# A planned attention stage: scoring steps ranked five tiles ahead, and the plan's durations replaced

## The chip, the core and the metric

The kernel runs on one core of a Trainium2 chip. Five engines work side by side, each with an instruction queue of its own that is worked off in order: TensorE (PE, with its weight loads shown apart as PEld), VectorE (DVE), ScalarE (ACT), GpSimd (POOL) and SyncE (SP, which here only issues transfers). They wait for each other through semaphores. The metric is the device time of one launch in microseconds, as the median of several runs.

## The reference

One transformer block with adaptive layer norm, on `x` of 2 batches x 2048 tokens x 256 features, all in f32:

```python
mod = (_silu(L0_c) @ L0_wmod).reshape(L0_c.shape[0], 6, 1, -1)
sa, ca, ga, sb, cb, gb = (mod[:, 0], ..., mod[:, 5])
ga = (2 * (ga >= 0) - 1) * jnp.maximum(jnp.abs(ga), 0.25)      # gb likewise
h = _layernorm(x, axis=-1) * (1 + ca) + sa
x = x + ga * attn(h, Wq, Wk, Wv, Wo)
h = _layernorm(x, axis=-1) * (1 + cb) + sb
x = x + gb * ffn(h, Wg, bg, Wt, bt, W1, b1, W2, b2)
```

`attn` is causal attention with two query heads of 128 that share one key and one value head, with rotary embedding on queries and keys. `ffn` is a mixture of eight experts (256 to 1024 to 256, GELU between): a softmax gate less a threshold of the token's own decides which experts a token goes to, and with which weight.

## The kernel before, in words

The work comes in two stages. `attention` (L203) does everything up to the experts' lists and a first piece of expert 0; `experts` (L1100) then runs loops on each engine over the experts' tokens, 256 at a time. The loops' main lines are L1219 (`h`, first product), L1245 (`g`, GELU) and L1210 (`y`, second product).

Attention is cut into 32 tiles of 128 tokens, which alternate between the batches in groups (4 tiles each three times, then 2, 1 and 1). A tile's number in that order is `r` (0.0 to 31.0). For each tile, `tile_steps` (L435) adds steps to a plan. In order, with the names that the profile shows:

- the load of `x` (L448, SP); its moments `sta`, `mva` (L423, L425, DVE) and `rstda` (L429, L430, POOL); the normalised `xn` (L459, DVE or POOL)
- `pt` (L468, PE): two transposes of `xn`; `hT` (L476, ACT, and L478, DVE): scaled and shifted on the way out of PSUM
- `pq` (L489, PE): queries, keys and values; `v` (L495, ACT); the rotation `t` (L505 to L520, DVE, the last add on DVE or POOL)
- `pr` (L527, PE): three transposes; `kT` and `qT` (L530, L532, ACT)
- `psc` (L543, L547, PE): scores of each head in chunks of 512 keys, with the mask added as a product; `s` and `mx` (L554, DVE): the scores copied out with their maximum; `nmx` (L561, DVE)
- `exp` (L570, ACT); `rd` (L603, L604, DVE)
- `ptr` (L616, PE): transposes of `s`, for two blocks of keys at a time; `pT` (L620, ACT); `pav` (L626, PE): times the values
- `aT` (L654, ACT); `po` (L660, PE): the output projection; `x` (L667, DVE): the residual; the store of `x` (L676, SP)
- the second layer norm `stf`, `mvf`, `rstdf`, `hx` (L423 to L430, L683, L686); `hp` (L693, POOL), stored by SP (L702)
- `hpT` (L714, a transposing transfer on SP) and `hT2` (L718, POOL or DVE), or in the last four tiles `ph` (L710, PE) and `hT2` (L725, ACT); `pl` (L730, PE): the gate's logits; `lg` (L738, DVE)

The steps to `nmx` are called a tile's front here, the rest its back. `gate_steps` (L751) adds for each group the gate's weights, a count of tokens (`pc`, L819) and the scatters into the experts' lists (L843, POOL). At rank 1000 come the steps that work ahead for expert 0 (`pha` L992, `pya` L1009, `yo` L1016 to L1021), the reading of the lists, and the gather that leads to `xT` (L941) for the loops' first item.

A step has one or more engines with a duration each, steps that it comes after, buffers that it takes and gives back, and a rank. `Plan.run` (L64) goes through time with these durations and lets every free engine take the ready step of lowest rank whose buffers are there; a step is ready 0.12 us after the last one that it comes after. What comes out is not a time but an order: the steps' instructions are issued in it, and each engine's queue keeps it on the chip, however long things take there. The core of it:

```python
for n in sorted(open_, key=lambda n: (self.steps[n][6], n)):
    ...
    idle = [(e, c) for e, c in zip(engs, costs) if free.get(e, 0.0) <= now]
    if not idle or ready[n] > now:
        continue
    eng, cost = idle[0]
    if any(self.room[r] < take.count(r) for r in take):
        continue
```

All steps of a tile have the rank `r`, through the local `add` (L443). The buffers that matter (L212): 6 of PSUM called `ps`, 9 of `x`, 16 of `s` (a late tile's two heads take 8), 3 of `pT`, 3 of `qT`.

Of the kernel before, what the change touches and what calls it, by code (L numbers as in the profile page):

```python
# [23 lines left out]
HS, NH = 128, 2  # L24
# [13 lines left out]
SC = 512  # L38
EPS = 1e-5
MASKED = -3.0e38  # L40
RES = 2


# [159 lines left out]
def attention(  # L203
# [5 lines left out]
    nc = tc.nc  # L209
# [19 lines left out]
    plan = Plan(room)  # L229
# [52 lines left out]
    def load(dst, src, kb, rank=first, **how):  # L282
# [9 lines left out]
    l_qkv = load(wqkv_sb, wqkvT.rearrange("(k p) f -> p k f", p=P), 512, rank=first - 1)  # L292
    l_rope = [
        load(rope_sb[:, ds(4 * q, 4)], rope.rearrange("(q n p) (z f) -> p q n z f", p=P, n=4, z=2)[:, q],
             256, rank=first if q == 0 else q * 8 - 7.5)
        for q in range(NT // 4)
    ]
# [5 lines left out]
    l_wg = load(wgt_sb, wgt.rearrange("(k p) e -> p k e", p=P), 9, rank=0.5)  # L303
# [7 lines left out]
    def load_expert(e):  # L311
# [13 lines left out]
        after=[s_sc], rank=first,  # L325
# [21 lines left out]
    m_T = plan.add("DVE", 0.3, by_feature_out, after=[m_pe], give=["ps"], rank=first)  # L347
# [70 lines left out]
    def moments(u, st, after, add):  # L418


        def stats():
            six = little([P, 6], "st", u)
            nc.vector.bn_stats(six, st["x"])  # L423
            st["mv"] = little([P, 2], "mv", u)
            nc.vector.bn_aggr(st["mv"], six)  # L425

        def rstd():
            st["rstd"] = little([P, 1], "rstd", u)
            nc.gpsimd.tensor_scalar(st["rstd"], st["mv"][:, 1:2], EPS, None, ALU.add)  # L429
            nc.gpsimd.tensor_tensor(st["rstd"], st["rstd"], neg_half, ALU.pow)  # L430

        n = add("DVE", 0.62, stats, after)
        return add("POOL", 0.85, rstd, [n])

    def tile_steps(b, i, r, group, g):  # L435
# [7 lines left out]
        def add(eng, cost, do, after=(), **how):  # L443
            return plan.add(eng, cost, do, after=after, rank=r, **how)

        def load_x():
            st["x"] = work([P, D], "x", u)
            nc.sync.dma_start(st["x"], x[b, ts(i, P), :])  # L448
# [3 lines left out]
        n_x = plan.add(  # L452
            "SP", 0.5, load_x, late=2.0, take=["x"], rank=first + early[r] if r in early else r
        )
        n_n = moments("a" + u, st, [n_x], add)

        def xn(eng):
            st["xn"] = work([P, D], "xn", u)
# [1 line left out]
                st["xn"], st["x"], st["mv"][:, 0:1], st["rstd"], ALU.subtract, ALU.mult  # L460
            )

        n_n = add(["DVE", "POOL"], [0.42, 1.3], xn, [n_n], take=["xn"])

        def turn():
            st["pt"] = ps_tile(f"pt{u}")
# [3 lines left out]
        def hT(k, eng):  # L470
            if "hT" not in st:
                st["hT"] = work([P, KD, P], "hT", u)
            scale_k, shift_k = modT[:, KD + k, b : b + 1], modT[:, k, b : b + 1]
            src, dst = st["pt"][:, ts(k, P)], st["hT"][:, k, :]
            if eng == "ACT":
                nc.scalar.activation(dst, src, AF.Identity, bias=shift_k, scale=scale_k)  # L476
            else:
                nc.vector.tensor_scalar(dst, src, scale_k, shift_k, ALU.mult, ALU.add)  # L478

        n_t = add("PE", 0.32, turn, [n_n], take=["ps"], give=["xn"])  # L480
        n_0 = add("ACT", 0.27, lambda: hT(0, "ACT"), [n_t, m_T], take=["hT"])
        n_1 = add(
            ["DVE", "ACT"], [0.41, 0.46], lambda eng: hT(1, eng), [n_t, m_T, n_0], give=["ps"]
        )

# [5 lines left out]
                    start=(k == 0), stop=(k == KD - 1),  # L491
                )

        n_q = add("PE", 1.75, qkv, [n_0, n_1, l_qkv], take=["ps"], give=["hT"])
        n_v = add("ACT", 0.27, lambda: nc.scalar.copy(v[:, i, :], st["pq"][:, 3 * HS :]), [n_q])  # L495
        ready_v[b, i] = n_v


        def rot(z):
            dst = st["t", z] = work([P, 3, HS], f"t{z}", u)  # L500
            table = rope_sb[:, i, z, :]
            src = st["pq"][:, : 3 * HS].rearrange("p (h j two) -> p h j two", h=3, two=2)
            d4 = dst.rearrange("p h (j two) -> p h j two", two=2)
            if z == 0:
                nc.vector.tensor_tensor(  # L505
                    d4, src,
                    table.unsqueeze(1).unsqueeze(3).to_broadcast([P, 3, HS // 2, 2]), ALU.mult,
                )
            else:
                t3 = table.unsqueeze(1).to_broadcast([P, 3, HS // 2])  # L510
                nc.vector.scalar_tensor_tensor(
                    d4[:, :, :, 0], src[:, :, :, 1], -1.0, t3, ALU.mult, ALU.mult
                )
                nc.vector.tensor_tensor(d4[:, :, :, 1], src[:, :, :, 0], t3, ALU.mult)

        n_r0 = add("DVE", 0.6, lambda: rot(0), [n_q, l_rope[i // 4]], take=["big"])
        n_r1 = add("DVE", 0.75, lambda: rot(1), [n_q, n_v, n_r0], give=["ps"])
        n_r = add(
            ["DVE", "POOL"], [0.58, 1.0],
            lambda eng: of[eng].tensor_tensor(st["t", 0], st["t", 0], st["t", 1], ALU.add),  # L520
            [n_r0, n_r1],
# [9 lines left out]
            st["qT"] = work([P, NH, P], "qT", u)  # L531
            nc.scalar.mul(st["qT"].rearrange("p h t -> p (h t)"), st["pr"][:, : NH * P], scale)  # L532

        n_t = add("PE", 0.48, turn_rot, [n_r], take=["ps"], give=["big"])
        n_k = add("ACT", 0.65, qT_out, [n_t], take=["qT"], give=["ps"])
        ready_k[b, i] = n_k


# [10 lines left out]
        def keep(h, c):  # L549
            w = min(SC, n - c * SC)  # L550
            s = st["s", h, c] = work([P, SC], "s", f"{u}_{h}_{c}")
            if ("mx", h) not in st:
                st["mx", h] = little([P, 4], "mx", f"{u}_{h}")
            nc.vector.tensor_scalar(  # L554
                s[:, :w], st["sc", h, c][:, :w], 1.0, None, ALU.mult, ALU.max,
                accum_out=st["mx", h][:, c : c + 1],
            )

        def top(h):
            st["nmx", h] = little([P, 1], "nmx", f"{u}_{h}")  # L560
            nc.vector.tensor_reduce(  # L561
                st["nmx", h], st["mx", h][:, :nch], AX.X, ALU.max, negate=True
            )
# [14 lines left out]
        for h in range(NH):  # L578
            kept = []
            for c in range(nch):  # L580
                w = min(SC, n - c * SC)
                n_s = add(
                    "PE", w * 0.0017 + (0.12 if c == nch - 1 else 0.0),
                    lambda h=h, c=c: score(h, c), n_keys + prev, take=["ps", "s"],
                    give=["qT"] if (h, c) == (NH - 1, nch - 1) else [],
                )
                prev = [n_s]
                kept.append(
                    add("DVE", 0.1 + w * 0.0013, lambda h=h, c=c: keep(h, c), [n_s], give=["ps"])
                )  # L590
            tops.append(add("DVE", 0.16, lambda h=h: top(h), kept))
        last_score[:] = prev
        n_e = {}
        for c in range(nch):
# [15 lines left out]
        def turn_p(c0, m):  # L610
            st["ptr"] = ps_tile(f"ptr{u}_{c0}")
            ptr = st["ptr", c0] = st["ptr"].rearrange("p (c h t) -> p c h t", c=2, h=NH)
            for j in range(m):
                for h in range(NH):
                    s = st["s", h, (c0 + j) * P // SC]
                    nc.tensor.transpose(ptr[:, j, h, :], s[:, ds((c0 + j) * P % SC, P)], ident)  # L616

        def pT_out(c0, m):
            pT = st["pT", c0] = work([P, 2, NH, P], "pT", f"{u}_{c0}")
            nc.scalar.copy(pT[:, :m], st["ptr", c0][:, :m])  # L620
# [12 lines left out]
        for c0 in range(0, i + 1, 2):  # L633
            m = min(2, i + 1 - c0)
            c = c0 * P // SC
            done = c0 + m == i + 1 or (c0 + m) * P % SC == 0
            n_t = add(
                "PE", 0.12 * 2 * m, lambda c0=c0, m=m: turn_p(c0, m), [n_e[0, c], n_e[1, c]],
                take=["ps"] + (["pav"] if c0 == 0 else []), give=["s", "s"] if done else [],
            )  # L640
            n_o = add(
                "ACT", 0.2 + 0.26 * m, lambda c0=c0, m=m: pT_out(c0, m), [n_t], take=["pT"],
                give=["ps"],
            )
            n_p.append(
                add(
                    "PE", 0.435 * m, lambda c0=c0, m=m: pav(c0, m),
                    [n_o] + n_p[-1:] + [ready_v[b, c0 + j] for j in range(m)], give=["pT"],
                )
            )  # L650
# [45 lines left out]


        by_dma = r < NTOK // P - 4
        n_f = add("POOL", 0.8, halves, [n_h], take=["hp"], give=["hx"] if by_dma else [])
        n_hp = add(  # L700
            "SP", 0.5,
            lambda: nc.sync.dma_start(  # L702
# [37 lines left out]
        if by_dma:  # L740
            n_t = add("SP", 1.3, turn_halves, [n_f, n_hp], late=2.2, take=["hpT"], give=["hp"])
            n_t = add(
                ["POOL", "DVE"], [0.65, 0.45], join_halves, [n_t], take=["hT2"], give=["hpT"]
            )
        else:
            n_t = add("PE", 0.32, turn_h, [n_h], take=["ps"])
            n_t = add("ACT", 0.38, hT2_out, [n_t, n_f], take=["hT2"], give=["ps", "hx"])
        n_t = add("PE", 0.5, logits, [n_t, l_wg], take=["ps"], give=["hT2"])
        return add("DVE", 0.17, logits_out, [n_t, l_bg], give=["ps"])

    def gate_steps(b, i0, m, q, group, after):  # L751
# [761 lines left out]
```

## Time and profile before

| | us |
|---|---|
| median of 3 runs | 1662.43 (1660.42 to 1665.69) |
| the profiled execution | 1666.95 |
| its span, first to last instruction | 1664.4 |
| of that, planned stage (to the last `pya`) | 476 |
| mean granted TensorE clock | 0.992 |

The profile comes from one execution. A row of its groups has the line, engine, operation, output and input with their shapes, the number of instructions; then busy time and the mean of one instruction in ns; then idle time of the engine just before them and what ended it. The ends of matmul records are modelled, so starts are the safer mark.

### The profile page before, as it was taken

The numbers are of one execution on the slowest core, as the hardware profiler recorded it, in microseconds if no ns is written. First come the engines' busy times: TensorE is split into PE (matmuls) and PEld (weight loads), VectorE is DVE, ScalarE is ACT, GpSimd is POOL, SyncE is SP. The second block draws the span as 40 slices with busy tenths as digits, with TensorE's granted clock in tenths as the row PEclk, the third lists the DMA queues.
The fourth block names the chain that finished last, engine by engine and source line by source line (L and its number), as shares of the span: only waits on it lengthen the run. The fifth ranks groups of instructions, "written<-read, shape, count | busy, mean of one in ns | idle before, by whom it ended". The sixth has DMA issues, their size and how long they took to land.

```text
span 1664.4 us, 26663 instructions
## 1 busy us (share of the span) xinstructions
PE 1616.1 (97%) x7610; PEld 1345.9 (81%) x7610; DVE 665.8 (40%) x2162; ACT 572.6 (34%) x1385; POOL 918.3 (55%) x1046
## 2 busy tenths in 40 slices
PE   8999999999989999999999999999999999999997
PEld 5667776767778888888888888788888888888886
DVE  7887756666432323222222322232232222222322
ACT  3555555555522222222222222222222222222222
POOL 4676424221137677656757765675676477644443
PEclk9999999999999999999999999999999999999998
DMA  5511111010033353335335333433533333333333
GB/s 159 169 52 43 48 30 36 20 46 17 20 85 60 68 115 57 62 57 105 57 64 106 57 65 59 97 57 59 108 57 61 57 58 60 65 57 57 64 57 48
DMA packets 181180, 108.96 MB, mean 65 GB/s; under 512 B 126272, under 2 KB 172480, under 8 KB 180992
## 3 DMA queue, kind: packets, MB, share of 16 engines
q0 software_dynamic: 41968, 46.83, 17.6%
q1 hardware_dynamic: 131280, 48.85, 12.9%
q10 hardware_dynamic: 7872, 12.58, 2.5%
q8 instruction: 25, 0.41, 0.1%
q14 instruction: 35, 0.29, 0.1%
HBM read 49.34 MB, written 31.86 MB: 49 GB/s over the span
## 4 chain that ended last, share of the span: by engine, by line
PE 69%; issue 1%; another core or an unknown queue 0%; DMA 0%; ACT 0%; POOLq 0%; DVE 0%; POOL 0%; DVEq 0%; ACTq 0%
PE h L1219 35%; PE y L1210 34%; DMA out<-yo,who 0%; ACT g L1245 0%; POOLq L1160 0%; DVE yo L1312 0%; DVE xT L941 0%; POOL out L1369 0%; DVE yb L1297 0%; DVEq L1509 0%; POOLq L1462 0%; POOLq L1369 0%; DVE who L1303 0%; POOLq L1464 0%
## 5 line engine op out<-in xcount | busy, mean ns | idle before, releaser
L1210 PE MATMUL y<-w,g 128*128 128x256 f32 x2640 | 658.1, 381 | 14.8 <-ACT g L1245 9.3
L1219 PE MATMUL h<-xT,w 128*128 128x256 f32 (+1 forms) x2752 | 660.9, 373 | 8.7 <-issue 8.5
L1245 ACT ACTIVATE g<-h,b_sb 128x256 f32<-128x256 f32 (+1 forms) x688 | 317.6, 465 | 865.6 <-PE h L1219 717.9
L1219 PEld LDWEIGHTS h<-xT,w 128*128 128x128 f32 x2752 | 516.4, 192 | 80.1 <-issue 8.9
L1210 PEld LDWEIGHTS y<-w,g 128*128 128x128 f32 x2640 | 499.5, 191 | 83.1 <-ACT g L1245 10.7
L1369 POOL DMA_INDIRECT out<-yo,who x172 | 282.9, 1645 | 232.7 <-DVE yo L1312 179.6
L1273 DVE COPY xT<-xp 128x512 uint16<-128x512 uint16 x172 | 67.7, 436 | 650.0 <-PE h L1219 477.4
L1359 POOL DMA_INDIRECT list<-new,to x216 | 230.9, 1069 | 93.6 <-issue 76.4
L1335 POOL DMA_INDIRECT xr<-feats,at x172 | 175.5, 1020 | 100.6 <-POOL at L1380 70.5
L626 PE MATMUL pav<-pT,v 128*128 128x256 f32 x544 | 143.1, 385 | 0.5 <-ACT pT L620 0.5
L543 PE MATMUL psc<-kT,qT 128*128 128x512 f32 (+3 forms) x320 | 142.5, 531 | 0.3 <-ACT pT L620 0.3
L626 PEld LDWEIGHTS pav<-pT,v 128*128 128x128 f32 x544 | 96.0, 190 | 31.4 <-issue 19.1
L1297 DVE TENSOR_TENSOR yb<-y,b_bc 128x256 f32<-128x256 f32 x165 | 62.7, 420 | 143.1 <-PE y L1210 135.4
L554 DVE TENSOR_SCALAR_CACHE_REDUCE s<-psc 128x512 f32<-128x512 f32 (+3 forms) x160 | 95.6, 604 | 55.1 <-PE psc L543 40.5
L570 ACT ACTIVATE s<-s,nmx 128x512 f32<-128x512 f32 (+3 forms) x160 | 103.8, 651 | 39.7 <-DVE nmx L561 39.5
L620 ACT COPY pT<-ptr 128x512 f32<-128x512 f32 (+1 forms) x144 | 76.1, 564 | 47.0 <-PE pav L626 33.9
L843 POOL DMA_INDIRECT list<-entry,place x40 | 42.4, 1059 | 79.5 <-DVE place L840 64.2
L1288 DVE SCALAR_TENSOR_TENSOR gate<-gb_bc,mcur,part 128x256 f32<-128x256 f32 x172 | 75.7, 482 | 3.0
L616 PEld LDWEIGHTS ptr<-ident,s 128*128 128x128 f32 x544 | 62.8, 141 | 16.6 <-ACT s L570 4.5
L616 PE MATMUL ptr<-ident,s 128*128 128x128 f32 x544 | 72.2, 274 | 1.7 <-ACT s L570 1.1
L543 PEld LDWEIGHTS psc<-kT,qT 128*128 128x128 f32 x320 | 57.6, 190 | 15.3 <-issue 7.3
L1380 POOL COPY at<-sheet 128x2 int32 x85 | 60.5, 712 | 13.2 <-DMA xp<-xr 13.2
(168 smaller groups left out, 1039.9 us busy)
## 6 DMA issues: line engine op xcount, KB each, us to landing
w<-in_w ACTq DMA_DIRECT2D x12, 1024.0 KB, 9.0
x<-in_x SPq DMA_DIRECT2D x32, 128.0 KB, 2.0
out<-x SPq DMA_DIRECT2D x32, 128.0 KB, 1.7
feats<-hp SPq DMA_DIRECT2D x32, 128.0 KB, 1.7
w<-in_w SPq DMA_DIRECT2D x4, 1024.0 KB, 7.9
list<-new,to POOLq DMA_INDIRECT x216
xr<-feats,at POOLq DMA_INDIRECT x172
out<-yo,who POOLq DMA_INDIRECT x172
```

Source lines behind the costliest of these rows:

```text
L543: nc.tensor.matmul(ps[:, :w], st["qT"][:, h, :], kT[:, ds(c * SC, w)], start=True, stop=not last)
L554: nc.vector.tensor_scalar(s[:, :w], st["sc", h, c][:, :w], 1.0, None, ALU.mult, ALU.max, accum_out=st["mx", h][:, c : c + 1],)
L570: nc.scalar.activation(s[:, :w], s[:, :w], AF.Exp, bias=st["nmx", h], accum_out=st["den"][:, h, c : c + 1],)
L616: nc.tensor.transpose(ptr[:, j, h, :], s[:, ds((c0 + j) * P % SC, P)], ident)
L620: nc.scalar.copy(pT[:, :m], st["ptr", c0][:, :m])
L626: nc.tensor.matmul(st["pav"][:, : NH * P], v[:, c0 + j, :], st["pT", c0][:, j].rearrange("p h t -> p (h t)"), start=(c0 + j == 0), stop=(c ...
L1210: last = pe.matmul(ys[c], gs[f % 4][:, ts(c, P)], weights[e][1][:, f, :], start=(f == 0), stop=(f == NF - 1),)
L1219: last = pe.matmul(hs[f % 4][:, :w], weights[e][0][:, k, ts(f, P)], xT[:, k, :w], start=(k == 0), stop=(k == KD - 1),)
L1245: act.activation(gs[f % 4][:, :w], hs[f % 4][:, :w], AF.Gelu_apprx_tanh, bias=b1_sb[:, at : at + 1],).then_inc(sem["act"], 1)
L1335: pool.indirect_dma_start(out=xr[:, ts(c, 2 * D)], out_offset=None, in_=feats, in_offset=bass.IndirectOffsetOnAxis(ap=at[:, c : c + 1], ax ...
L1359: pool.indirect_dma_start(out=lists[e], out_offset=bass.IndirectOffsetOnAxis(ap=to[:, j : j + 1], axis=0), in_=new[:, j, :], in_offset=Non ...
L1369: pool.indirect_dma_start(out=rows, out_offset=bass.IndirectOffsetOnAxis(ap=who[:, c : c + 1], axis=0), in_=yo[:, c, :], in_offset=None, b ...
```

## The change

Two things. A second helper, `lead`, adds a tile's front steps at rank `r - LEAD` with `LEAD = 5`; the load of `x` and the back keep the rank `r`. And eleven of the durations that the plan uses are other numbers. No step's instructions are changed. The steps `v`, `rot(0)`, `rot(1)`, the add, `turn_rot` and `qT_out`, left out below, also go from `add` to `lead`, with the durations they had. (Line numbers behind the constant are one higher in the new kernel, and five higher behind `lead`.)

```diff
+LEAD = 5
...
         def add(eng, cost, do, after=(), **how):
             return plan.add(eng, cost, do, after=after, rank=r, **how)
+        def lead(eng, cost, do, after=(), **how):
+            return plan.add(eng, cost, do, after=after, rank=r - LEAD, **how)
...
-        n_n = moments("a" + u, st, [n_x], add)
+        n_n = moments("a" + u, st, [n_x], lead)
...
-        n_n = add(["DVE", "POOL"], [0.42, 1.3], xn, [n_n], take=["xn"])
+        n_n = lead(["DVE", "POOL"], [0.42, 1.3], xn, [n_n], take=["xn"])
...
-        n_t = add("PE", 0.32, turn, [n_n], take=["ps"], give=["xn"])
-        n_0 = add("ACT", 0.27, lambda: hT(0, "ACT"), [n_t, m_T], take=["hT"])
-        n_1 = add(
+        n_t = lead("PE", 0.24, turn, [n_n], take=["ps"], give=["xn"])
+        n_0 = lead("ACT", 0.46, lambda: hT(0, "ACT"), [n_t, m_T], take=["hT"])
+        n_1 = lead(
...
-        n_q = add("PE", 1.75, qkv, [n_0, n_1, l_qkv], take=["ps"], give=["hT"])
+        n_q = lead("PE", 1.75, qkv, [n_0, n_1, l_qkv], take=["ps"], give=["hT"])
...
-                n_s = add(
-                    "PE", w * 0.0017 + (0.12 if c == nch - 1 else 0.0),
+                n_s = lead(
+                    "PE", w * 0.00168 + (0.06 if c == nch - 1 else 0.0),
...
-                    add("DVE", 0.1 + w * 0.0013, lambda h=h, c=c: keep(h, c), [n_s], give=["ps"])
+                    lead("DVE", 0.1 + w * 0.0013, lambda h=h, c=c: keep(h, c), [n_s], give=["ps"])
-            tops.append(add("DVE", 0.16, lambda h=h: top(h), kept))
+            tops.append(lead("DVE", 0.16, lambda h=h: top(h), kept))
...
-                "PE", 0.12 * 2 * m, lambda c0=c0, m=m: turn_p(c0, m), [n_e[0, c], n_e[1, c]],
+                "PE", 0.11 * 2 * m, lambda c0=c0, m=m: turn_p(c0, m), [n_e[0, c], n_e[1, c]],
...
-                "ACT", 0.2 + 0.26 * m, lambda c0=c0, m=m: pT_out(c0, m), [n_t], take=["pT"],
+                "ACT", 0.16 + 0.215 * m, lambda c0=c0, m=m: pT_out(c0, m), [n_t], take=["pT"],
...
-        n_f = add("POOL", 0.8, halves, [n_h], take=["hp"], give=["hx"] if by_dma else [])
+        n_f = add("POOL", 0.65, halves, [n_h], take=["hp"], give=["hx"] if by_dma else [])
...
-                ["POOL", "DVE"], [0.65, 0.45], join_halves, [n_t], take=["hT2"], give=["hpT"]
+                ["POOL", "DVE"], [0.66, 0.58], join_halves, [n_t], take=["hT2"], give=["hpT"]
...
-        n_t = add("PE", 0.5, logits, [n_t, l_wg], take=["ps"], give=["hT2"])
+        n_t = add("PE", 0.37, logits, [n_t, l_wg], take=["ps"], give=["hT2"])
```

More of the change, by code (lines that the diff above doesn't have):

```diff
@@ L492, in qkv @@
                 )
-        n_q = add("PE", 1.75, qkv, [n_0, n_1, l_qkv], take=["ps"], give=["hT"])
-        n_v = add("ACT", 0.27, lambda: nc.scalar.copy(v[:, i, :], st["pq"][:, 3 * HS :]), [n_q])
+        n_q = lead("PE", 1.75, qkv, [n_0, n_1, l_qkv], take=["ps"], give=["hT"])
+        n_v = lead("ACT", 0.27, lambda: nc.scalar.copy(v[:, i, :], st["pq"][:, 3 * HS :]), [n_q])
         ready_v[b, i] = n_v
@@ L514, in rot @@
                 nc.vector.tensor_tensor(d4[:, :, :, 1], src[:, :, :, 0], t3, ALU.mult)
-        n_r0 = add("DVE", 0.6, lambda: rot(0), [n_q, l_rope[i // 4]], take=["big"])
-        n_r1 = add("DVE", 0.75, lambda: rot(1), [n_q, n_v, n_r0], give=["ps"])
-        n_r = add(
+        n_r0 = lead("DVE", 0.6, lambda: rot(0), [n_q, l_rope[i // 4]], take=["big"])
+        n_r1 = lead("DVE", 0.75, lambda: rot(1), [n_q, n_v, n_r0], give=["ps"])
+        n_r = lead(
             ["DVE", "POOL"], [0.58, 1.0],
@@ L532, in qT_out @@
             nc.scalar.mul(st["qT"].rearrange("p h t -> p (h t)"), st["pr"][:, : NH * P], scale)
-        n_t = add("PE", 0.48, turn_rot, [n_r], take=["ps"], give=["big"])
-        n_k = add("ACT", 0.65, qT_out, [n_t], take=["qT"], give=["ps"])
+        n_t = lead("PE", 0.48, turn_rot, [n_r], take=["ps"], give=["big"])
+        n_k = lead("ACT", 0.65, qT_out, [n_t], take=["qT"], give=["ps"])
         ready_k[b, i] = n_k
```

## The prediction, made before the changed kernel ran

> **What bounds the kernel now.** I read first the page's busy shares, then the stretches of time, then the waits of TensorE alone, then its timeline.
>
> ```profile
> PE 1616.1 (97%) x7610; PEld 1345.9 (81%) x7610; DVE 665.8 (40%) x2162; ACT 572.6 (34%) x1385; POOL 918.3 (55%) x1046
> ```
>
> TensorE (PE) has work nearly all the time. The stretches split the span at its stages (columns: length; busy time of each engine with instructions; granted clock, DMA share, GB/s):
>
> ```profile
> 20.00:80.00 60.00, 57.89 (x274) 38.55 (x272) 52.58 (x196) 31.89 (x98) 34.06 (x55) 1.00 0.42 128
> 80.00:125.00 45.00, 44.17 (x215) 30.93 (x216) 39.20 (x150) 25.49 (x74) 33.04 (x46) 1.00 0.21 57
> ...
> 300.00:400.00 100.00, 99.40 (x471) 69.76 (x470) 63.42 (x247) 56.43 (x153) 26.07 (x36) 1.00 0.13 32
> 400.00:450.00 50.00, 47.64 (x260) 38.05 (x259) 26.08 (x121) 30.29 (x75) 7.12 (x11) 1.00 0.05 14
> ...
> 476.00:481.00 5.00, 0.53 (x3) 0.13 (x1) 2.39 (x8) 0.00 (x0) 0.28 (x1) 1.00 0.07 7
> 481.00:1664.00 1183.00, 1152.82 (x5392) 1013.11 (x5392) 343.04 (x944) 317.60 (x688) 730.16 (x757) 0.99 0.39 69
> ```
>
> The planned part ends at 476 us. The 1183 us behind it are the experts' loops, which the plan does not order. So the change can only act on 476 us, in which VectorE (DVE) is second, at 88% and 87% in the first two rows.
>
> How much of the 476 us is TensorE waiting? A matmul record ends late (its end is modelled), so I took starts. In the timeline an f32 matmul of 256 columns is two instructions 0.216 us apart, one of 512 two of 0.429, a transpose of 128 one of 0.109. What a start lies behind that is waiting. Between 20 and 476 us there are 22 such gaps over 0.13 us, 10.3 us together: nine ahead of the transposes of scores `ptr` (L616), 3.17; one ahead of `ph` (L710), 2.49; three ahead of the logits `pl` (L730), 1.34; four ahead of `pt` (L468), 1.31; two ahead of `pav` (L626), 0.80; two ahead of `pq` (L489), 0.73; one ahead of `psc` (L543), 0.46. The list of TensorE's waits from 15 to 476 us names their releasers, and the timeline shows the largest:
>
> ```profile
> PE ph L710 <- DVE hx L686: 2.3, 1, 2.3
> PE ptr L616 <- ACT s L570: 1.1, 1, 1.1
> PE pl L730 <- DVE hT L718: 0.5, 1, 0.5
> PE pav L626 <- ACT pT L620: 0.5, 1, 0.5
> ```
>
> ```profile
> 431.51 1.88 PE L543 MATMUL psc<-kT,qT 128*128 128x512 f32 x4
> 433.23 0.22 PE L547 MATMUL psc<-maskb,identb 128*128 128x128 bf16 x1
> 435.78 0.41 PE L710 MATMUL ph<-ident,hx 128*128 128x128 f32 x2 [2.33 <-DVE hx L686]
> 436.02 1.15 PE L616 MATMUL ptr<-ident,s 128*128 128x128 f32 x9
> ```
>
> The reader is to see that the last tile's scores end at 433 us and nothing is left to fill the wait for what follows. The rows that the chains below are made of:
>
> ```profile
> L570 ACT ACTIVATE s<-s,nmx 128x512 f32<-128x512 f32 x112 | 80.0, 716 | 36.8 <-DVE nmx L561 36.6
> L554 DVE TENSOR_SCALAR_CACHE_REDUCE s<-psc 128x512 f32<-128x512 f32 x112 | 76.3, 685 | 47.2 <-PE psc L543 40.5 <-PE psc L547 4.0 <-PE pc L822 1.0
> ...
> L620 ACT COPY pT<-ptr 128x512 f32<-128x512 f32 x128 | 70.4, 588 | 39.9 <-PE pav L626 28.7 <-PE ptr L616 9.3 <-PE pc L822 1.1
> ...
> L476 ACT ACTIVATE hT<-pt,modT 128x128 f32<-128x128 f32 x55 | 22.2, 459 | 17.2 <-PE pt L468 12.9 <-PE pq L489 4.3
> ```
>
> **A rule against the rows.** The Trainium skill, page "Perfetto Trace Analysis", section "Identifying the Most-Contended Engine", says that matmul busy time is a bad measure of headroom on TensorE, and that the busy share of weight loads (with the share of peak arithmetic) should be used. Here weight loads are busy 69.76 of 100 us. Read as headroom that is 30%, about 140 of the 456 us, and a better order could bring tens of us. The starts say 10.3 us. I take the starts: they contain no modelled end. For this change the rule's other half holds, since the 97% alone would have hidden the 10.3.
>
> **The change, part by part.** No operation is added or removed: 1787 rows in TensorE's order before and after. The planner's choices of engine move ten: four `hT` from ScalarE (0.459) to VectorE (0.407), three adds of L520 from VectorE (0.588) to POOL (0.998), three joins of L718 from VectorE (0.540) to POOL (0.664). That is 1.6 us more on POOL's chains in all, 1.8 us less on VectorE; both lie in chains whose cover I give below, so they cost nothing.
>
> **The costs.** They are only what the planner believes. Lowered on TensorE: 544 transposes by 0.01 (5.4 us), the score's last term by 0.06 for 64 (3.8), 0.13 for 32 logits (4.2), 0.08 for 32 `pt` (2.6), 0.00002 for 69632 score columns (1.4): 17.4 us of TensorE time that the plan had believed in and that does not exist. TensorE is therefore sooner at its next step than the plan of before expected. The copy `pT_out` goes from 0.72 to 0.59 (row: 0.588), `hT` on ScalarE from 0.27 to 0.46 (row: 0.459).
>
> **The lead.** What is worth reading is the cover: TensorE's own work, at the spacings above, that stands in its order between the step which starts a chain and the step which needs its end. I worked it out for every tile in both orders.
>
> - Last score to first `ptr`: median 3.9 us before, the smallest 0.22 (last tile) and 2.05; after 19.9, smallest 4.4. The chain is 0.685 + 0.083 + 0.148 (maximum) + 0.716 + 0.189, 1.8 us, and about 0.5 of hand-overs (estimate: 0.2 from the end of a matmul's columns to the reader's start, 0.29 from a ScalarE end at 430.36 to the matmul at 430.65). The nine gaps, 3.17 us, go.
> - `po` to `ph`: 1.83 us for tile 15 of batch 0 before, smallest after 6.5. The chain took 3.9 in the timeline (431.7 to 435.6). The 2.49 go.
> - `po` to `pl`: median 13.4 before, 15.1 after, smallest 11.25 and 11.66. Of the 1.34 I leave 0.3.
> - `ptr` to `pav`: under the 1.1 us that the chain needs (0.588 + 0.5) 7 times of 144 before, 8 after. The 0.80 stay. The single one ahead of `psc`: 0.2 of 0.46.
> - `pt` to `pq` and `pq` to `pr` get shorter: medians 6.9 to 2.65, and 11.1 to 4.55. The chains are 2 x 0.459 + 0.5 = 1.4, with covers of mostly 1.7, and 0.554 + 0.35 + 0.35 + 0.998 + 0.5 = 2.75, with 3.28 at least. I leave the 1.31 and 0.73 of `pt` and `pq` as they are.
>
> So 3.3 us of the 10.3 stay, and 7.0 go.
>
> **Queues that the led steps pass.** They issue no DMA. On SP the load of `x` keeps its rank, behind out stores and `hp` of earlier tiles, as before; tile r+9 can only load once tile r's `hx` has freed its buffer, and in the new order `po` of tile r, with some 6 us behind it, stands at least 19 us of TensorE work ahead of the `pt` of tile r+9 in the tiles that I followed (9 to 15). On POOL the led `rstd`, `xn` and adds go ahead of list scatters (L843, 1.06 each) and `hp` copies; those feed `pl`, which gained 1.7 of cover, and the lists. On ScalarE `exp` waits longer, with 16 us of extra cover. Buffers: between the last writer of a `ps` slot and its next one stand at least 0.91 us of TensorE's work in the new order, 0.44 in the old; the 16 `s` slots are full, but a slot's last `ptr` stands ahead of the next `psc` in TensorE's own order.
>
> **The hand-over at 476 us.** It is 4.67 us between the last `pya` and the first `h`. VectorE's results (from 476.57) and `xT` (478.04 to 478.80) end last. The last tile's `pl`, count and total stand 1.75 us of TensorE work later in the new order against the same end; they lead over the last scatter (463.03) and SP's transpose (472.63) to `xT`. The stretch 474 to 476 has a DMA share of 0.62 and the next 0.00, so the data were there about 2.1 us ahead of 478.04. 2.1 less 1.75 is hidden; if it is not, each us costs one. I take 0.3 (ends 0 and 2).
>
> **Sum.** 7.0 less 0.3 is 6.7. The profiled execution took 1666.95 us (span 1664.4 and 2.55 around it), 4.5 above the median 1662.43 of the three runs; 1660.2 for it, and 1655.7 for a median.
>
> What the trace cannot show: the experts' stage has waits for no engine (ScalarE `g` "remote", 27.6 us in 15 pieces, up to 5.0). All programs shift by a few instructions. Nearest row 5.0 either way for one of them; I take 0 and keep 3 on both sides.
>
> **The rivals.**
>
> - The gap moves (no visible change). `pt` and `pq` now stand as close as the chain allows, in all 32 tiles. 0.1 us each at two places is 6.4 us: 1662. For it: covers of 1.7 against 1.4, with an `exp` of 0.9 possibly in ScalarE's queue. Against: before, `pt` at 1.4 to 1.9 showed no regular gap.
> - VectorE becomes the bound while the lead is built (slower). By 165 us of TensorE work three more tiles have their front done, of about 7 us on VectorE each, and two fewer their back, of about 4.9: 11 us more in the stretch where it is at 87%. It decides from about 95%, when each further us is a wait: all 11 exposed less 6.7 is 1666.7. Against: summing VectorE's durations in its order up to what TensorE needs, that sum stays 4.2 to 6.9 us under TensorE's through the first 110 us of before, and 12 to 24 us after (from 25 us on), since the early tiles' backs wait.
> - The list's chain misses the hand-over by 3 us: 1658.7.
> - All 10.3 us go: 1652.
>
> That the lead does nothing is out: the order shows it at two to five tiles.
>
> **Numbers.** The forecast has 0.50, all of it gone 0.08, the gap moved 0.19, the hand-over 0.05, VectorE 0.18. Over 0.3% (5.0 us, about what a measurement here can tell from no change) faster, under 1657.4: 0.46 of the forecast and the 0.08. Within: 0.04, 0.19 and 0.05. Slower: 0.18. The range reaches from everything gone with a little of the 3 us, 1651, to VectorE's case, 1667.
>
> **What would show it.** Right: the 2.3 us wait of `ph` on `hx` is gone, `ptr` waits no more on `exp`, PE busy over 49 in 400 to 450, the first `h` near 474 us. Wrong: gaps ahead of `pq` or `pr` in most tiles; VectorE over 95% in 80 to 165 with PE under it; or `xT` waiting on its DMA at the hand-over.

## The result, and the profile after

| | before | changed |
|---|---|---|
| median of 12 runs each, same chip | 1665.68 (1657.08 to 1670.07) | 1656.30 (1646.31 to 1664.08) |
| ratio to before, 95% interval | | 0.9945 (0.9919 to 0.9971) |
| profiled execution (its span) | 1666.95 (1664.4) | 1649.47 (1647.1) |
| last `pya` | 476.15 | 466.88 |
| first `h` | 481.04 | 472.59 |
| first `h` to the end of the span | 1183.4 | 1174.5 |

The change is faster by 0.55% (0.29 to 0.81), 9.2 us on the median of before; 6.7 had been forecast. The two profiled executions lie 17.5 us apart, and that is not the change's size: the changed one was 6.8 below its own median, and the experts' stage, which the plan doesn't order, differs by 8.9 in them. What the change did is read from the first `h`, 8.45 us sooner.

The page's first row, and the same stretches of time as before (columns: length; busy time of each engine with instructions; granted clock, DMA share, GB/s):

```profile
PE 1610.2 (98%) x7610; PEld 1341.6 (81%) x7610; DVE 669.0 (41%) x2160; ACT 572.5 (35%) x1381; POOL 921.5 (56%) x1052
```

```profile
20.00:80.00 60.00, 59.92 (x281) 40.25 (x280) 51.80 (x183) 34.01 (x105) 30.08 (x47) 1.00 0.36 109
80.00:125.00 45.00, 44.92 (x217) 30.96 (x216) 38.33 (x145) 26.48 (x80) 27.48 (x42) 1.00 0.26 71
125.00:165.00 40.00, 39.71 (x189) 27.28 (x188) 32.91 (x125) 23.98 (x68) 24.71 (x37) 1.00 0.17 47
...
300.00:400.00 100.00, 100.00 (x486) 71.83 (x485) 61.49 (x230) 55.35 (x149) 22.65 (x32) 1.00 0.12 31
400.00:450.00 50.00, 50.00 (x275) 41.32 (x274) 27.84 (x125) 29.67 (x70) 11.23 (x17) 1.00 0.07 22
450.00:466.50 16.50, 16.50 (x80) 14.36 (x79) 7.90 (x42) 4.10 (x9) 3.04 (x3) 1.00 0.07 20
466.50:476.00 9.50, 4.17 (x12) 3.13 (x11) 3.96 (x11) 0.47 (x1) 3.19 (x2) 0.82 0.45 144
```

TensorE is busy for all of 300 to 466.5 us, 59.92 of the first 60 shown. VectorE has 86%, 85% and 82% in the first three rows and nowhere the 95% that the prediction took as its mark. The last row holds the end of the planned stage, the wait ahead of the first `h` and 3.4 us at half clock behind it (0.82 over the row). All that TensorE's list of waits from 15 to 485 us still names:

```profile
PE h L1224 <- DVEq L1328: 5.3, 1, 5.3
PE pl L735 <- PE psc L552: 0.3, 1, 0.3
PE pr L532 <- POOL t L525: 0.2, 1, 0.2
```

By the starts, as in the prediction, 4 gaps over 0.13 us are left of 22, 1.31 us of 10.30: two ahead of `pr` (0.61), one each ahead of `pl` (0.45) and `po` (0.24). With the waits below 0.13 us counted too (each start against the smallest spacing of its shape), what starts lie behind fell from 28.3 to 18.1 us. From the first matmul to the last `pya` the stage took 9.9 us less (459.8 against 469.7), of which 0.6 is lost to a later first matmul (7.04 against 6.43).

The hand-over from the planned stage to the loops took more. The timelines of VectorE and, for the gather that fetches the first item's tokens, of GpSimd (POOL), first after, then before:

```profile
458.66 0.76 DVE L1021 TENSOR_TENSOR yo<-pya,b_bc 128x256 f32<-128x256 f32 x2 [0.22 <-PE pya L1014]
459.45 0.69 DVE L1024 TENSOR_TENSOR yo<-yo,size_a 128x512 f32<-128x512 f32 x1
...
461.94 0.22 DVE L1065 SCALAR_TENSOR_TENSOR next_at<-next_at,flag,sheet 128x2 int32<-128x2 int32 x1
462.44 0.98 POOL L931 DMA_INDIRECT g_sb_r_next<-feats,next_at  x1 [6.99 <-DVE next_at L1065]
467.30 0.76 DVE L1021 TENSOR_TENSOR yo<-pya,b_bc 128x256 f32<-128x256 f32 x2 [5.13 <-PE pya L1014]
...
469.63 0.76 DVE L946 COPY xT<-sign_p_next 128x512 uint16<-128x512 uint16 x2 [0.77 <-DMA sign_p_next<-g_sb_r_next]
```

```profile
467.29 0.22 DVE L1060 SCALAR_TENSOR_TENSOR next_at<-next_at,flag,sheet 128x2 int32<-128x2 int32 x1
468.53 0.99 POOL L926 DMA_INDIRECT g_sb_r_next<-feats,next_at  x1 [4.41 <-issue]
470.94 0.76 DVE L1016 TENSOR_TENSOR yo<-pya,b_bc 128x256 f32<-128x256 f32 x2 [3.43 <-issue]
...
478.04 0.76 DVE L941 COPY xT<-sign_p_next 128x512 uint16<-128x512 uint16 x2
```

Before, `next_at`, which holds the tokens of the loops' first item, came ahead of the first result `yo`. Now it stands behind it and the gates `size_a` in VectorE's queue. Against the last `pya` it is 3.9 us later (461.75 is 5.13 ahead of it, before 467.09 was 9.06 ahead), and the gather is 3.2 us later (4.44 ahead, before 7.62). So `xT` waits 0.77 us for its transfer, and the gap ahead of the first `h`, from the start of the last `pya` to its own, is 5.71 instead of 4.89.

### The profile page after: what moved, and what is told of

The parts are those of the page before. It is cut to its first block, busy times and chain, and to the rows that moved or that the text cites. A ratio compares the mean times of both kernels' runs of the same rounds, so it can differ in the third digit from the quotient of the medians.

```text
span 1647.1 us, 26672 instructions
## 1 busy us (share of the span) xinstructions
PE 1610.2 (98%) x7610; PEld 1341.6 (81%) x7610; DVE 669.0 (41%) x2160; ACT 572.5 (35%) x1381; POOL 921.5 (56%) x1052
## 4 chain that ended last, share of the span: by engine, by line
PE 96%; DMA 1%; issue 1%; another core or an unknown queue 1%; DVE 0%; POOL 0%; ACT 0%; POOLq 0%; SPq 0%; DVEq 0%; ACTq 0%
PE y L1215 35%; PE h L1224 35%; PE pav L631 7%; PE psc L548 7%; PE ptr L621 4%; PE pq L494 3%; PE po L665 2%; PE pha L997 1%; PE pl L735 1%; PE pr L532 1%; PE pya L1014 0%; PE pt L473 0%; DMA wm<-in_wmod 0%; DMA out<-yo,who 0%
## 5 line engine op out<-in xcount | busy, mean ns | idle before, releaser
L1364 POOL DMA_INDIRECT list<-new,to x216 | 227.0, 1051 | 93.6 <-issue 71.0
L621 PE MATMUL ptr<-ident,s 128*128 128x128 f32 x544 | 78.5, 273 | 0.0
L494 PE MATMUL pq<-wqkv_sb,hT 128*128 128x512 f32 x128 | 62.4, 612 | 0.1
```

The source lines that it names most:

```text
L494: nc.tensor.matmul(st["pq"], st["hT"][:, k, :], wqkv_sb[:, k, :], start=(k == 0), stop=(k == KD - 1),)
L1364: pool.indirect_dma_start(out=lists[e], out_offset=bass.IndirectOffsetOnAxis(ap=to[:, j : j + 1], axis=0), in_=new[:, j, :], in_offset=Non ...
```

## The experiments

All are read in the same way: the gaps over 0.13 us between TensorE's starts from 20 us to the last `pya`, from one trace each. A ratio is to the kernel before on the same chip. The medians of before were 1646.1 to 1668.1 on the chips used, so times from different chips are compared by ratio only. Edits are shown against the changed kernel, in part.

| kernel | gaps, us (number) | last `pya` | gap ahead of first `h` | first `h` | ratio (95%) |
|---|---|---|---|---|---|
| before, first trace | 10.30 (22) | 476.15 | 4.89 | 481.04 | |
| before, second trace | 11.60 (22) | 478.96 | 4.84 | 483.81 | |
| changed | 1.31 (4) | 466.88 | 5.71 | 472.59 | 0.9945 (0.9919 to 0.9971) |
| changed, second trace | 1.91 (4) | 467.31 | 5.70 | 473.00 | 0.9924 (0.9905 to 0.9943) |
| lead alone | 3.90 (8) | 469.73 | 4.85 | 474.57 | 0.9944 (0.9925 to 0.9963) |
| durations alone | 8.91 (17) | 477.40 | 4.85 | 482.25 | 0.9986 (0.9969 to 1.0003) |
| LEAD = 1 | 8.22 (16) | 475.21 | 4.84 | 480.05 | 0.9961 (0.9944 to 0.9978) |
| LEAD = 2 | 8.16 (16) | 474.81 | 4.85 | 479.66 | 0.9947 (0.9934 to 0.9960) |
| LEAD = 8 | 4.17 (11) | 469.33 | 4.69 | 474.02 | one run |
| lead, TensorE's durations | 3.16 (5) | 467.33 | 6.98 | 474.31 | one run |
| lead, other durations | 4.16 (5) | 469.99 | 4.83 | 474.82 | one run |
| `next_at`, `xT` ahead | 1.38 (4) | 467.55 | 5.94 | 473.50 | 0.9926 (0.9909 to 0.9944) |
| and the gather ahead | 1.62 (4) | 466.51 | 4.14 | 470.65 | 0.9930 (0.9915 to 0.9945) |

The three kernels with one run took 1647.10 (LEAD = 8), 1652.71 and 1651.07 us, against one run of 1668.10 of the kernel before. Single runs of the changed kernel lie up to 18 us apart (1646.31 to 1664.08), so these three are read by their traces alone.

**The lead alone.** The eleven numbers, in the durations of eight steps, are those of before; two of the eight:

```diff
-        n_t = lead("PE", 0.24, turn, [n_n], take=["ps"], give=["xn"])
+        n_t = lead("PE", 0.32, turn, [n_n], take=["ps"], give=["xn"])
...
-                "PE", 0.11 * 2 * m, lambda c0=c0, m=m: turn_p(c0, m), [n_e[0, c], n_e[1, c]],
+                "PE", 0.12 * 2 * m, lambda c0=c0, m=m: turn_p(c0, m), [n_e[0, c], n_e[1, c]],
```

> The lead of five with the durations of before. Theory (the lead closes the scores' waits, the durations the short ones): no gap ahead of `ptr` or `ph` (smallest cover from last score to first `ptr` is 3.2 us in this order, `po` to `ph` 5.2), but gaps ahead of `pt`, `pq` and `pav`, where this order has covers of 0.22, 0.89 and 0 to 0.9; together 2.5 to 4.5 us between 20 us and the end of the planned stage, so 2 us slower than the changed kernel, about 0.996 of before. Rival one (true durations do it, the lead hardly matters): gaps of 7 us or more, about 0.999. Rival two (the gain lies in the experts' stage, from moved code): the planned stage ends within 2 us of before, at 474 to 476.

TensorE's waits in the same stretch:

```profile
PE h L1224 <- DVEq L1328: 4.5, 1, 4.5
PE pav L631 <- ACT pT L625: 0.7, 1, 0.7
PE pl L735 <- POOL hT L723: 0.7, 1, 0.7
PE pl L735 <- DVE hT L723: 0.5, 1, 0.5
PE pt L473 <- POOL xn L464: 0.5, 1, 0.5
PE po L665 <- ACT aT L659: 0.2, 1, 0.2
```

No wait of `ptr` or `ph` is left: the 5.66 us that these two had are the lead's. The rest, 3.90, is ahead of `pl` (1.48), `pav` (1.09), `pt` (0.61), `po` (0.51) and `psc` (0.21). The theory's range held, and `pt` and `pav` are among its places, but the largest part is ahead of `pl`, which it did not name. The last `pya` at 469.73 is outside rival two's 474 to 476, and 3.90 outside rival one's 7 or more. The ratio is that of the changed kernel and not the 0.996 of the theory, with an interval that reaches there; the 2.6 us of gaps between the two kernels are seen in the traces only, and 0.86 of them are given back by the shorter hand-over.

**The durations alone**, with one edit:

```diff
-LEAD = 5
+LEAD = 0
```

> The new durations with LEAD = 0, so all steps of a tile at one rank as before. Theory (the lead closes the scores' waits): the cover from last score to first `ptr` is 0.6 us at its smallest and six are under 2.6, so gaps ahead of `ptr` stay, 2 to 4 us; the one ahead of `ph` is closed, since the plan now leaves 4.5 us there; total 3.5 to 6 us, about 0.997 of before. Rival one (true durations do it): total under 2 us, all of the gain, 0.9945. Rival two (experts' stage): planned stage ends at 474 to 476 us.

The gaps are 8.91 us, more than the theory's 6: `ptr` keeps seven (4.26). The two largest of TensorE's waits after that of the first `h`, and its timeline at the last tile:

```profile
PE ptr L621 <- ACT s L575: 2.3, 3, 1.5
PE pl L735 <- ACT hT L730: 0.7, 1, 0.7
```

```profile
432.62 0.44 PE L715 MATMUL ph<-ident,hx 128*128 128x128 f32 x2
433.78 0.61 PE L735 MATMUL pl<-wgt_sb,hT 128*128 128x9 f32 x4 [0.73 <-ACT hT L730]
434.25 0.31 PE L621 MATMUL ptr<-ident,s 128*128 128x128 f32 x1
436.10 0.98 PE L621 MATMUL ptr<-ident,s 128*128 128x128 f32 x7 [1.54 <-ACT s L575]
```

The wait of `ph` is closed as expected (0.14 is left of 2.49), but the 2.6 us came back two steps on, at `pl` (0.89) and `ptr` (1.74), since the last scores still end just ahead with nothing to fill in. That was left out of the expectation. Without the lead the new durations give 0.14%, with an interval that holds no change.

**How long a lead?**

> The changed kernel with LEAD = 1 in place of 5. Theory (the front must be several tiles ahead): covers from last score to `ptr` are as before (0.86 the smallest, median 4.3) and `po` to `ph` is 1.75 again, so the gap ahead of `ph` comes back at about 2.5 us and `ptr` keeps 1 to 3; total 4 to 7 us, about 0.997. Rival one (durations do it): total under 2 us, 0.9945.

> The changed kernel with LEAD = 2. Theory (a gap goes where its cover exceeds its chain): last score to `ptr` has 2.27 us at its smallest against the 2.3 of the chain, `po` to `ph` 3.8 against 3.9, so `ptr` keeps at most 0.5 us and `ph` 0.2; but `pt` (0.66) and `ptr` to `pav` (0.33, 0.44, 0.55) get short covers and 1 to 2 us of gaps; total 1.5 to 3.5 us, between LEAD = 1 (8.2) and LEAD = 5 (1.3). Rival (only a lead of five reaches far enough): 6 us or more.

> The changed kernel with LEAD = 8. Theory (the covers are there from five on; buffers bound the lead): smallest cover from last score to `ptr` 6.2 us, `po` to `ph` 4.8, `pt` to `pq` 1.3, so gaps of 1 to 2.5 us together, the last `pya` within 1.5 us of LEAD = 5. Rival (five is a fine balance, and more lead starves the backs): 4 us or more.

LEAD = 1 leaves 8.22 us and LEAD = 2 8.16, at five 1.31, at eight 4.17. For one tile the theory, with 4 to 7, had the direction but was 1.2 short, and the gap at the last tile came ahead of `ptr` (2.06), not of `ph`. For two, where it had 1.5 to 3.5, it was wrong: the short covers ahead of `pav` cost 1.54, as expected, but three gaps ahead of `pr` (2.44) and three ahead of `ptr` (2.14) came on top. GpSimd's timeline ahead of one of the gaps with LEAD = 2 (`pr` starts at 170.51):

```profile
168.31 1.09 POOL L848 DMA_INDIRECT list<-entry,place  x1 [0.19 <-issue]
169.43 1.02 POOL L525 TENSOR_TENSOR t<-t,t 128x384 f32<-128x384 f32 x1
```

The rotation's last add ends these waits. Here its input was ready on VectorE at 166.8 us, but the add stood behind list scatters in GpSimd's queue, and at the other two behind gathers on GpSimd or the gate's steps on VectorE. The covers from `pq` to `pr` are 5.4, 3.0 and 6.4 us at these gaps, while covers of 2.6 and 3.0 elsewhere show none. So a cover that is compared with the chain's own durations misses what else stands in the queues of the chain's engines.

At eight the gaps were 4.17 us against at most 2.5, with small ones in seven kinds of step; that is the number of the rival, whose reason was not tested. So by the gaps the lead has to be several tiles, and what is left behind it depends on how steps happen to meet; that five is the best value is not shown, only that it left the least of the four. The ratios do not separate two tiles from five; the last section says what may hide it.

**Which durations?** Two halves of the table of durations, each with LEAD = 5.

> LEAD = 5 with the new durations of TensorE's own steps alone (`pt`, scores, `ptr`, `pl`), the other engines' as before. Theory (a step of TensorE that the plan holds for longer than it is makes the chains beside it look covered): `ptr` to `pav` has 0.97 us at its smallest, so no gap ahead of `pav`; the gaps ahead of `pt` or `pl`, whose chains end on ScalarE, VectorE and GpSimd, stay at up to 2 us; total 1.5 to 3 us. Rival (the other engines' durations matter): 3.5 us or more, with about 1 us ahead of `pav`, as with the lead alone (3.9).

> LEAD = 5 with the new durations of ScalarE's, GpSimd's and VectorE's steps alone (`hT`, `pT`, `hp`, the join of `hT2`), TensorE's as before. Theory: `ptr` to `pav` is 0 us at its smallest again, so about 1 us ahead of `pav` stays; `pt` to `pq` is 1.3 and more, so the 0.61 us of that chain goes; total 1.5 to 3 us. Rival (the other engines' durations matter most): under 1.5 us, as in the changed kernel.

With TensorE's durations no gap ahead of `pav` remains; with the others' alone one of 0.89 stays, at the same place as with the lead alone (438.7 and 438.4 us). That part of the theory holds. Its reason, that the plan held transposes for 10% longer than they are and so believed the copy of `pT` covered, is argued: the other three of TensorE's durations changed with them. The gap ahead of `pt` went with the others' durations, as expected. But neither half is in the expected 1.5 to 3 us: 3.16 with two ahead of `pl` (2.23), and 4.16 with three ahead of `pr` (2.39). The last 2 to 3 us go only with both. The long gap ahead of the first `h` in the first half (6.98) goes with a wait of `xT` for its transfer of 2.2 us, against 0.77 in the changed kernel; why it was longer was not followed.

**The hand-over, first try.** In the plan the first result comes after `next_at`, the last one after `xT`. The steps that lead to `next_at` and `xT` are also set up ahead of the work for expert 0, so they come first among steps of the same rank:

```diff
-        low("DVE", 1.5, result, [n, n_g, l_b2], give=["ps", "size"])
+        low("DVE", 1.5, result, [n, n_g, l_b2, n_behind if k < AHEAD - 1 else n_next], give=["ps", "size"])
```

> The changed kernel with two more dependencies in the plan: the first result of the work ahead (`yo`, 0) comes after `next_at`, and the last (`yo`, 1) after `xT`. Nothing else moves on TensorE. Theory (the hand-over of the changed kernel hangs on `next_at`, which stands behind 3.2 us of `yo` and gates on VectorE's queue, and then on VectorE's last work): `next_at` starts at about 458.6 instead of 461.75, `xT` lies ahead of the last `yo`, and the gap ahead of the first `h` falls from 5.5 us to about 4.2; total 1.3 us less than the changed kernel, 0.9937 of before. Rival (the first `h` waits for what other engines do at the entry of the loops, register loads and branches): the gap stays at 5.2 to 5.5.

`next_at` did come earlier, and the gap did not shrink (5.94). VectorE's and GpSimd's timelines:

```profile
459.24 0.22 DVE L979 SCALAR_TENSOR_TENSOR next_at<-next_at,flag,sheet 128x2 int32<-128x2 int32 x1
...
469.10 0.77 DVE L946 COPY xT<-sign_p_next 128x512 uint16<-128x512 uint16 x2 [6.56 <-DMA sign_p_next<-g_sb_r_next]
```

```profile
461.76 1.12 POOL L931 DMA_INDIRECT g_sb_r_next<-feats,next_at  x1 [5.63 <-DVE size_a L1007]
```

The gather starts 2.3 us after `next_at` had ended (459.46). The profile names `size_a`, which the gather doesn't use. In GpSimd's order four loads of counts into registers stand ahead of the gather; loads don't count as busy, and they can begin once the counts are there (459.12). The rival's number held, but not its reason: there was a second wait behind the first.

**The hand-over, second try.** One more dependency: GpSimd's register loads come after the gather.

```diff
-    low("POOL", 1.0, hold("POOL", nc.gpsimd, [skip, 0, E, 2 * E]), [n_total])
+    low("POOL", 1.0, hold("POOL", nc.gpsimd, [skip, 0, E, 2 * E]), [n_total, n_gather])
```

> The kernel with `next_at` and `xT` ahead, and one more dependency: GpSimd loads its counts into registers after the gather of the first item, not ahead of it. Theory (the gap of 5.9 us stayed since the gather waited for these loads, 2.6 us after the counts, and not for `next_at`): the gather starts about 0.4 us after `next_at`, some 2 us earlier, `xT` lies about at the last `pya`, VectorE's last result ends last, and the gap falls to 3.9 to 4.4 us; 1.7 us less than the kernel with `next_at` and `xT` ahead, a ratio of about 0.991 to 0.994. Rival (VectorE's traffic at the shared memory delays the gather's descriptors): the gather starts at 461.5 or later again, the gap stays at 5.5 to 6.

```profile
458.66 0.99 POOL L931 DMA_INDIRECT g_sb_r_next<-feats,next_at  x1 [3.58 <-DVE next_at L979]
```

```profile
458.17 0.22 DVE L979 SCALAR_TENSOR_TENSOR next_at<-next_at,flag,sheet 128x2 int32<-128x2 int32 x1
...
465.96 0.76 DVE L946 COPY xT<-sign_p_next 128x512 uint16<-128x512 uint16 x2 [4.33 <-DMA sign_p_next<-g_sb_r_next]
466.92 0.76 DVE L1042 TENSOR_TENSOR yo<-pya,b_bc 128x256 f32<-128x256 f32 x2 [0.20 <-PE pya L1035]
```

The gather follows `next_at` by 0.27 us, `xT` is done ahead of the last `yo`, and the gap is 4.14, 1.56 less than in the changed kernel beside it. The register loads were the wait, and not VectorE's traffic: VectorE works on `yo` and `size_a` right behind `next_at` here too, and the gather starts all the same. The kernel before had this wait as well: its gather starts 2.5 us after the counts (465.99 to 468.53), 1.02 after `next_at` had ended. The time does not resolve it: 0.9930 (0.9915 to 0.9945) against 0.9924 (0.9905 to 0.9943) for the changed kernel. This version beats the kernel before; that it beats the changed one is seen in the trace only.

**Both kernels once more.**

> The kernel before once more, for a second trace of its stages. Theory (the planned stage is fixed by the order, the experts' stage differs from execution to execution): the gaps of the planned stage are again 9 to 11 us at the same places; the time from the first `h` to the end is not the 1183.4 of the first trace but anything from 1155 to 1185. Rival (the changed kernel's experts' stage is really 9 us shorter): it lies about 9 us above that of the changed kernel in the run beside it.

> The changed kernel once more, beside the kernel before. Theory: four gaps of 1.3 us in the planned stage, a last `pya` 9 us sooner than the kernel before, a gap ahead of the first `h` about 0.8 us longer; a ratio of 0.9945 to 0.9955. Rival (experts' stage): its experts' stage is again 9 us under that of the kernel before, and the ratio is under 0.9925 or the planned stage has gained nothing.

The gaps are at the same places to within 1.3 us in both kernels. The experts' stage is 1159.8 in the kernel before and 1161.1 in the changed one: nothing of the 8.9 us of the first pair remains. So the rival is out, although the ratio, 0.9924, meets one of its two marks (under 0.9925) and lies just under the theory's 0.9945, which its interval almost holds (up to 0.9943). The medians of this pair are 10.5 us apart and the first `h` 10.8, so the planned stage and the hand-over account for it.

## Why the prediction was right

- **The waits for scores (`ptr`, 3.17, and `ph`, 2.49).** Both gone, by the lead, as the covers had said. The lead alone takes them; the durations alone close `ph`'s but leave 4.26 ahead of `ptr`. TensorE is busy for all of 400 to 450 us, and the first `h` is at 472.59 where 474 was named.
- **`pl`.** 0.3 was to stay of 1.34; 0.45 stays.
- **What I left standing.** I left 1.31 ahead of `pt`, 0.73 of `pq`, 0.80 of `pav` and 0.2 of `psc`: all went, and 0.61 ahead of `pr` and 0.24 of `po` came new. This is the step that was off: 3.3 us were to stay and 1.31 did. For `pav` I took 1.1 us as the need of its chain. Where a gap stands, cover and gap together give the need: 0.22 and 0.62, 0.65 and 0.18 in the trace of before, 0 and 0.89 with the lead alone, so 0.84 to 0.89; in the changed kernel covers of 0.65 to 0.91 stand with waits of at most 0.03. The trace of before had said so: seven covers under 1.1 and only two gaps. For `pt` I reasoned on the chain behind it, while two of its four gaps (0.69 us) end with the step ahead, `xn`, and the others with `qT` (0.37) and the residual `x` (0.26). And I had given the new durations no term of their own; beside the lead they take 2 to 2.6 us (3.90 with the lead alone, 1.31 and 1.91 with both).
- **The hand-over.** 0.3 us was taken, 0.82 came (5.71 less 4.89), inside the range of 0 to 2 but for another reason. I had 1.75 us of later lists against 2.1 of slack. The last scatter, though, is only 0.6 us later against the last `pya` (12.53 ahead of it, before 13.12); the rest is `next_at` behind 3.1 us of VectorE's own queue (458.66 to 461.75). Nor had I followed GpSimd's: its register loads held the gather before the change, are hidden behind that wait in the changed kernel, and take its place once it is gone. `xT` waiting on its transfer was named as a sign of being wrong, and it is in the trace: on the hand-over the mechanism was wrong, and its cost small.
- **The sum.** 7.0 less 0.3 was to be 6.7. In the first pair of traces the first `h` is 8.45 us sooner. Against the forecast that is 2.0 more of gaps and, on balance, 0.9 of smaller waits, which I had not counted, less 0.6 for the later first matmul and 0.5 more at the hand-over. In the second pair it is 10.8 (483.81 less 473.00), mainly since the kernel before lost 1.3 us more ahead of one `pl` and 1.7 to a slow stretch that is told of below. That the forecast of a median, 1655.7, lies 0.6 from the measured 1656.30 is luck: three runs had given 1662.43 for before, twelve gave 1665.68, and the gain was larger by nearly as much.
- **The rivals.** Gaps moved to `pt` and `pq`: not one is there, and ahead of `pr` stand two. VectorE as the bound: 86% at most, with TensorE busy beside it. The misses at the hand-over: 0.8 us, not 3. The rival that comes nearest is the one in which all 10.3 us go: 9.0 did.
- **The rule on weight loads.** Their busy time in 300 to 400 us went from 69.76 to 71.83 us while TensorE's gaps over 0.13 us went from three (1.09 us) to none. The 28% that is still free of loads was not headroom for an order of steps; the starts had the right size.

## What to carry to other kernels

Where an order made by a planner runs on an engine that is nearly full, work out the cover of each chain in both orders, and calibrate the need of a chain by the trace (cover plus gap where a gap stands, and the smallest covers without one), not by adding durations up. Look, too, at what else stands in the queues of the chain's engines. Here a front that runs several tiles ahead took the waits for a long chain; true durations took short ones beside the lead, and gave nothing that the times could show without it. The end of a stage needs working of its own: follow the last result through every queue that it passes, register loads included, since here one wait of some 3 us hid another of 2.3.

## What the runs showed of the hardware

**A gap can cost more than itself.** In the second trace of the kernel before, the 2.50 us wait of `ph` (434.4 to 436.9) is followed by this (one us a row; the granted clock is the number ahead of the last two, which are of the DMA):

```profile
437.00:438.00 1.00, 1.00 (x6) 1.00 (x7) 0.00 (x0) 1.00 (x5) 0.45 (x1) 0.54 0.00 0
438.00:439.00 1.00, 1.00 (x7) 1.00 (x6) 0.00 (x0) 1.00 (x5) 0.00 (x0) 0.50 0.38 131
...
440.00:441.00 1.00, 1.00 (x9) 1.00 (x8) 0.00 (x0) 0.00 (x0) 0.00 (x0) 0.76 0.00 0
441.00:442.00 1.00, 1.00 (x11) 1.00 (x10) 0.37 (x3) 0.00 (x0) 0.00 (x0) 1.00 0.00 0
```

Fifteen starts of transposes come at 0.213 us behind the one before instead of 0.109; with those at both edges that is 1.7 us on top of the wait. In the first trace the same gap was followed by a clock of 1.00. The Trainium skill, page "TensorE: Matmul & The Clock Gate", section "Part 1: The HAM clock gate (the "warmup" mystery)", says that an idle window of about 3.4 us halves the array's clock and a busy one brings it back, and that the window runs freely, so that the same kernel meets it at different points. The 0.50, the return after about 3.4 us (437.1 to 440.5) and the difference between two executions agree; that 2.5 us of idle time were enough is shorter than the page has. (With the durations alone, gaps of 0.89 and 1.74 us at the last tile, with some 0.6 us of work between, were followed by 3.4 us at half clock too.) For the change it means that the wait of `ph` cost 2.5 or 4.2 us, by execution. The hand-over paid it in all thirteen traces: behind the first `h`, six to twelve instructions of 256 columns come at twice their spacing, about 0.21 us lost on each, so 1.3 to 2.5 us.

**One wait and two groups of times.** With the durations alone, five runs took 1639.2 to 1640.3 us and seven 1645.4 to 1648.2, with none between. On the chips of this run and of the second pair, six traces have a gap of 3.8 to 4.3 us ahead of one `h` at 1023 to 1036 us, at the change to another expert, and an experts' stage of 1159.8 to 1163.3 us. Two have none there (LEAD = 1 and 2), and 1155.0 and 1155.9. Both kinds, each in the ten us from 0.7 ahead of the first of the expert's weights, first with the gap (`next_at` and `xT` ahead), then without (LEAD = 1):

```profile
1020.00:1030.00 10.00, 6.14 (x21) 4.78 (x21) 3.19 (x9) 1.03 (x3) 5.85 (x5) 0.83 1.04 223
```

```profile
1026.60:1036.60 10.00, 10.00 (x49) 8.79 (x48) 3.19 (x9) 2.84 (x6) 5.86 (x5) 1.00 1.01 220
```

The profile names no engine for the gap. The weights are on their way in both (DMA share 1.04 and 1.01), and one packet of each instruction queue falls close by in both, so neither makes the wait by itself; the cause stays open.

Sorted by these groups after the fact, the runs of four kernels on one chip follow the first `h`:

| kernel | first `h` | lower group, median (runs) | upper group, median (runs) |
|---|---|---|---|
| durations alone | 482.25 | 1639.61 (5) | 1647.28 (7) |
| LEAD = 1 | 480.05 | 1637.39 (8) | 1644.30 (3) |
| lead alone | 474.57 | 1632.29 (2) | 1639.73 (4) |
| `next_at`, `xT` ahead | 473.50 | 1631.04 (3) | 1636.72 (3) |

The traced runs with the gap are of the upper group, the one without it (LEAD = 1) of the lower. All five runs with LEAD = 2 lie within 1.7 us (1637.0 to 1638.8), and the traced one has no gap. So it is likely, though not shown, that this wait makes the groups, and that LEAD = 1 and 2 have lower ratios than their first `h` lets expect because more of their runs are without it (8 of 11 and all 5, against 2 of 6 for the changed kernel). Against a difference of 5 to 8 us, 1.6 us at the hand-over cannot be seen in a median of a few runs.

The first pair has other waits in the experts' stage, mostly ahead of `y` and 0.7 to 2.5 us long. Its gaps over 0.25 us are 21.4 us before and 14.4 changed, against 5.2 and 5.3 in the second pair, and they make up most of the 8.9 us by which the first pair differs behind the first `h`.
